# The first requests of a one-core LSTM kernel: four steps of x, a part of Wx, then the other four steps

## The chip, the cores and the metric

The kernel runs on one core of a Trainium2 chip. The metric is the device time of one execution in microseconds (us), lower is better. A core has a matrix engine (TensorE, PE in the profile, with PEld for its weight loads), a vector engine (VectorE, DVE), a scalar engine (ScalarE, ACT), a general one (GpSimd, POOL) and a synchronising one (SyncE, SP). SP, ACT and POOL also issue the transfers (DMAs) from main memory.

## The reference

A sequence x of 64 steps for 32 sequences (256 features) goes through an LSTM with 256 hidden units, then through a feed-forward network with weights of plus and minus one, and the result is added to x. All is float32.

```python
xW = jnp.einsum('ntd,dg->ntg', x, Wx) + b
def step(carry, xw_t):
    prev_h, prev_c = carry
    a = xw_t + prev_h @ Wh
    i = jax.nn.sigmoid(a[:, :Hd])
    f = jax.nn.sigmoid(a[:, Hd:2 * Hd])
    o = jax.nn.sigmoid(a[:, 2 * Hd:3 * Hd])
    g = jnp.tanh(a[:, 3 * Hd:])
    next_c = f * prev_c + i * g
    next_h = o * jnp.tanh(next_c)
    return ((next_h, next_c), next_h)
...
h = jnp.concatenate([x, -x], axis=-1)
h = s0 * _conn_dense(k0, h)
h = jax.nn.relu(h) * 2
h = s1 * _conn_dense(k1, h)
h = jax.nn.relu(h) * 2
h = s2 * _conn_dense(k2, h)
...
x = x + _L0_ffn_ref(_L0_cond_ref(x, cond_1024, ...), ...)
```

Here x of the second part is the hidden state of every step, and Hd is 256.

## The kernel before, in words

**The steps of the LSTM.** The 64 steps are a recurrence: each needs the hidden state of the one before. For each step TensorE multiplies the state with Wh (`gates_from_h`, L301 to 312: 32 matrix instructions on the trace, since a float32 product is two passes), ScalarE and VectorE do the cell (`cell_step`, L319 to 342), and VectorE turns the new state round for the next product. While the cell is worked out, TensorE does work that does not depend on it: in the first 21 steps the products of x with Wx for later steps (`x_products`, L272), then the feed-forward network of steps already done (`ffn_block`, L585, and `last_block`, L417). So TensorE always has a queue of work, and the program's order on it is fixed by the loop over t at the end of the function.

**Layout.** A step's gates lie on 128 partitions as four groups (q) of 32 sequences, each with 64 of the 256 hidden units. Wx and Wh are each 256 rows by 1024 columns and stand in SBUF as two chunks of 128 rows (k = 0, 1) and four slots of 256 columns. `GATES = (3, 0, 1, 2)` says which gate of the reference stands in which slot: slot 0 is g, slots 1, 2 and 3 are i, f and o. `load_gates` (L118) asks for some slots of some chunks; with two engines given, each asks for one half of the partitions. `load_x` (L88) asks for eight steps of x (a half of a block of 16), or a part of them, in four transfers, one for each q. `turn_x` (L226) turns them round on VectorE.

**The start.** This is where the change lies. VectorE zeroes `warm` (L108, 40 words a partition), `idle` (L110, 512 bf16 values, done as 256 words) and the two tiles `b_row` (L116) into which the bias goes. TensorE first multiplies `idle` with itself: two products that put zeros into the two banks of the gates (L641) and `WARM_UP` = 8 into a bank that nothing reads (L643, `p_idle`). Then come, in this order on TensorE:

1. `x_part` (L242, its matmul is L246) for steps 0 to 7 with chunk 0 and slots 1 and 2: the first pass;
2. the same with slots 0 and 3: the second pass;
3. the bias, spread over the partitions by a product (`copy_bias`, L658), which needs `b_row`;
4. chunk 1 with all slots for steps 0 to 7; after each two steps VectorE moves the sum, with the bias, to SBUF (`evict_x`, L262);
5. the products for steps 8 to 11, which need the second eight steps of x, turned on VectorE after the first `evict_x`;
6. the first recurrence, which needs Wh and the turned initial state `h_first` (L679).

**The requests.** SP and ACT ask for the large tiles, in the order of the program: the first eight steps of x (q0 and q2 by SP, q1 and q3 by ACT), Wx chunk 0 (slots 1 and 2 in one request by SP, slot 0 and slot 3 by ACT), Wx chunk 1 in the same way, the second eight steps of x, then Wh. The requests of these two engines share eight semaphores in turn. A request takes the semaphore of the one that stands eight places ahead of it, so it waits on its engine until that one has landed, and what is behind it on the same engine waits too. POOL asks for `h_first`, for three pieces of the bias and for the three scales, and then computes with the scales (L169 to L183). After these SP alone asks for more of x (L155), k0 (L162) and k1 (L198).

Of the kernel before, what the change touches and what calls it, by code (L numbers as in the profile page):

```python
# [32 lines left out]
F32 = mybir.dt.float32  # L33
# [8 lines left out]
def lstm_ffn(ctx: ExitStack, tc: tile.TileContext, x, cond, wx_d, wh_d, b_d, k0_d, k1_d, k2_d, s0_d, s1_d, s2_d, out):  # L42
    nc = tc.nc
    P = 128
# [3 lines left out]
    NQ = 4  # L48
    HQ = H // NQ
# [3 lines left out]
    SB = 16  # L53
    NB = T // SB
    TB = SB * N
# [6 lines left out]

    FIRST_CHORE = 2
    W2_STEP = 24
    WARM_UP = 8

    SUM_STEP = 28

    const = ctx.enter_context(tc.tile_pool(name="const", bufs=1))
# [12 lines left out]
    def act(shape, dtype, name):  # L82
        return apool.tile(shape, dtype, tag="act", name=name)
# [4 lines left out]
    def load_x(i, half, engines, part=slice(0, SB // 2)):  # L88
        if part.start == 0:
            xq[i, half] = xpool.tile([P, SB // 2, HQ], F32, tag="x", name=f"x{i}_{half}")  # L90
        t0 = i * SB + half * (SB // 2)
        for q in range(NQ):
            engines[q % len(engines)].dma_start(
                out=xq[i, half][q * N : (q + 1) * N, part],
                in_=x[:, t0 + part.start : t0 + part.stop, ts(q, HQ)],
            )
# [5 lines left out]
    wx = wpool.tile([P, 2, G], F32, tag="wx", name="wx")  # L102
# [2 lines left out]
    w2 = const.tile([P, 2, FC1, P], F32R, name="w2")  # L105

    warm = const.tile([P, 40], F32, name="warm")
    nc.vector.memset(warm, 0.0)  # L108
    idle = const.tile([P, 512], mybir.dt.bfloat16, name="idle")
    nc.vector.memset(idle, 0.0)  # L110

    first = warm[:, 4 : 4 + N]
    nc.vector.memset(first[:1], 1.0)
# [4 lines left out]
    def load_gates(t, w_d, slots, engines, chunks=slice(0, 2)):  # L118

        w_rows = w_d.rearrange("(p b) g -> p b g", b=2)  # L120
        s0, n, g0 = slots[0], len(slots), GATES[slots[0]]
        if len(engines) == 1:
            halves = [slice(0, P)]
        else:
            halves = [slice(0, P // 2), slice(P // 2, P)]
        for engine, half in zip(engines, halves):
            engine.dma_start(
                out=t[half, chunks, s0 * H : (s0 + n) * H], in_=w_rows[half, chunks, g0 * H : (g0 + n) * H]
            )


    both = [nc.sync, nc.scalar]
    load_x(0, 0, both)
    for k in range(2):
        load_gates(wx, wx_d, (1, 2), [nc.sync], slice(k, k + 1))
        for slot in (0, 3):
            load_gates(wx, wx_d, (slot,), [nc.scalar], slice(k, k + 1))
    load_x(0, 1, both)
    load_gates(wh, wh_d, (1, 2), both)
    load_gates(wh, wh_d, (0,), [nc.scalar])  # L140
    load_gates(wh, wh_d, (3,), [nc.sync])

    nc.scalar.activation(warm[:, 1:2], warm[:, :1], AF.Sigmoid)
    h_first = const.tile([P, HQ], F32, name="h_first")
    nc.gpsimd.dma_start(out=h_first, in_=cond.rearrange("n (q j) -> q n j", q=NQ))
    b_rows = b_d.rearrange("(o g h) -> o g h", o=1, g=4)
    nc.gpsimd.dma_start(out=b_row[0][:1, :1], in_=b_rows[:, 3:])
    nc.gpsimd.dma_start(out=b_row[0][:1, 1:], in_=b_rows[:, :1])
    nc.gpsimd.dma_start(out=b_row[1][:1], in_=b_rows[:, 1:3])
    scales = []  # L150
    for i, s_d in enumerate((s0_d, s1_d, s2_d)):
        s = const.tile([P, 1], F32, name=f"s{i}")
# [73 lines left out]
    def turn_x(i, half, part=slice(0, SB // 2)):  # L226
        if part.start == 0:
            xT[i, half] = act([P, SB // 2, 2, N], F32, f"xT{i}_{half}")
        nc.vector.transpose(
            xT[i, half][:, part], xq[i, half][:, part].rearrange("p t (j b) -> p t b j", b=2)  # L230
        )
# [405 lines left out]
    outputs = deque()  # L637

    p_idle = ps_f.tile([P, TB], F32, tag="pf", name="p_idle")
    for g in gate_banks:  # L640
        nc.tensor.matmul(g, idle[:, :P], idle, start=True, stop=True)  # L641
    for n in range(WARM_UP):
        nc.tensor.matmul(p_idle, idle[:, :P], idle, start=True, stop=True)  # L643
    turn_x(0, 0, slice(0, SB // 4))
    turn_x(0, 0, slice(SB // 4, SB // 2))
    for i in range(4):
        load_bits(i)
    for half in range(2):
# [53 lines left out]
    for t in range(T):  # L702
# [22 lines left out]
        else:  # L725
            if t >= FIRST_CHORE and chores:
                part = chores.popleft()()
# [40 lines left out]
```

## Time and profile before

| what | value |
|---|---|
| median of 3 runs | 312.36 us (312.21 to 312.55) |
| the profiled execution's own time | 312.31 us |
| its span on the core | 310.5 us |
| TensorE busy | 304.5 us, 98% of the span |
| share of TensorE in the chain that ended last | 97% |
| first instruction on TensorE | at 1.24 us |
| first product of x | at 5.44 us |
| first product of the recurrence | at 16.60 us |

The times of one instruction and of its group come from the profiled execution, counted from the start of its span. A matmul is pipelined, so its time in the profile (634 ns for a product of zeros) is longer than the distance from one to the next (0.43 us); for the length of a run of matmuls the distance counts. The chain of work that ended last is followed back from the last instruction: what stands on it sets the end. A weight load can start before the matmul ahead of it is done.

### The profile page before, as it was taken

How to read it: one execution, taken by the hardware profiler on the slowest of the kernel's cores; microseconds unless marked ns; L12 is line 12 of the kernel's file. 1: busy time of each engine (PE TensorE's matmuls, PEld its weight loads, DVE VectorE, ACT ScalarE, POOL GpSimd, SP SyncE). 2: the span in 40 equal slices, each digit the busy share in tenths (PEclk: the TensorE clock that was granted, in tenths of full speed). 3: DMA queues.
4: the chain of work that ended last, by engine and by line, in shares of the span. 5: the costliest groups of instructions: out<-in, count | busy, mean ns of one | idle time of the engine just before them, and what ended most of it. 6: DMA issues, size and time to landing. Idle time of an engine off the chain costs nothing.

```text
span 310.5 us, 9798 instructions
## 1 busy us (share of the span) xinstructions
PE 304.5 (98%) x4138; PEld 242.7 (78%) x4138; DVE 178.1 (57%) x530; ACT 142.0 (46%) x512; POOL 6.6 (2%) x24
## 2 busy tenths in 40 slices
PE   8999999999999999999999999999999999999994
PEld 4888888788777777777777777777777777899993
DVE  2566767777673444355754445567554434698543
ACT  0225566774564543435633434355443333886220
POOL 5300000000000000000000000000000000000000
PEclk9999999999999999999999999999999999999999
DMA  6874001142000000000010000000310000131002
GB/s 192 206 196 99 5 19 38 36 95 65 3 2 0 2 2 0 3 2 0 2 38 22 14 3 0 2 2 13 92 34 2 3 0 2 31 79 27 2 0 69
DMA packets 30587, 10.89 MB, mean 35 GB/s; under 512 B 27720, under 2 KB 29768, under 8 KB 30544
## 3 DMA queue, kind: packets, MB, share of 16 engines
q1 hardware_dynamic: 27136, 8.66, 11.2%
q10 hardware_dynamic: 3168, 1.57, 2.0%
q8 instruction: 32, 0.52, 0.7%
q0 software_dynamic: 240, 0.04, 0.1%
q14 instruction: 11, 0.09, 0.1%
HBM read 8.16 MB, written 2.10 MB: 33 GB/s over the span
## 4 chain that ended last, share of the span: by engine, by line
PE 97%; DVE 1%; ACT 0%; issue 0%; ACTq 0%
PE p L617 30%; PE gates L305 20%; PE px L246 18%; PE p L591 8%; PE po L604 7%; PE gates L452 4%; PE po L561 2%; PE r L452 2%; PE x L452 2%; PE p L479 2%; PE p_idle L643 1%; PE gates L641 0%; DVE a_7l L362 0%; DVE o L388 0%; PE p_bias L658 0%
## 5 line engine op out<-in xcount | busy, mean ns | idle before, releaser
L305 PEld LDWEIGHTS gates<-wh,hist 128*32 128x32 f32 x2016 | 54.6, 109 | 22.3 <-issue 13.4
L305 PE MATMUL gates<-wh,hist 128*32 128x192 f32 x2016 | 68.1, 275 | 0.0
L246 PE MATMUL px<-wx,xT 128*32 128x256 f32 (+1 forms) x1168 | 60.5, 353 | 0.1
L322 ACT ACTIVATE sig<-gates 128x128 f32<-128x128 f32 x64 | 17.7, 277 | 80.6 <-PE gates L305 80.4
L246 PEld LDWEIGHTS px<-wx,xT 128*32 128x32 f32 x1168 | 42.4, 110 | 11.3 <-DVE c_first L652 0.7
L326 DVE TENSOR_TENSOR kept<-sig,c 128x64 f32<-128x64 f32 x63 | 14.2, 225 | 50.0 <-ACT sig L322 49.7
L332 ACT ACTIVATE th<-c 128x64 f32<-128x64 f32 x64 | 16.4, 257 | 31.4 <-DVE c L330 31.4
L334 DVE TENSOR_TENSOR h<-sig,th 128x64 f32<-128x64 f32 x64 | 14.4, 225 | 20.7 <-ACT th L332 20.7
L262 DVE TENSOR_TENSOR xg<-px,bias 128x512 f32<-128x512 f32 x32 | 21.2, 671 | 2.8 <-PE px L246 2.3
L316 ACT COPY gates<-xg 128x192 f32<-128x192 f32 x64 | 20.0, 313 | 1.3 <-DVE xg L262 1.3
L591 PE MATMUL p<-hhi,w 128*128 128x512 f32 x48 | 19.3, 402 | 0.0
L591 PE MATMUL p<-hlo,w 128*128 128x512 f32 x48 | 19.1, 398 | 0.0
L339 DVE STREAM_TRANSPOSE hist<-h 128x64 f32<-128x64 f32 x64 | 15.7, 245 | 2.4
L330 DVE TENSOR_TENSOR c<-kept,new 128x64 f32<-128x64 f32 x64 | 14.4, 224 | 2.2
L324 ACT ACTIVATE sig<-gates 128x64 f32<-128x64 f32 x64 | 14.9, 233 | 0.1
L323 ACT ACTIVATE cand<-gates 128x64 f32<-128x64 f32 x64 | 14.0, 218 | 0.0
L328 DVE TENSOR_TENSOR new<-sig,cand 128x64 f32<-128x64 f32 x64 | 13.9, 217 | 0.0
L317 ACT COPY gates<-xg 128x64 f32<-128x64 f32 x64 | 13.0, 203 | 0.0
L591 PEld LDWEIGHTS p<-hhi,w 128*128 128x128 f32 x48 | 9.0, 188 | 2.2
L591 PEld LDWEIGHTS p<-hlo,w 128*128 128x128 f32 x48 | 9.0, 188 | 2.0
L211 ACT ACTIVATE w<-bits,nsgn,sgn 128x1024 fp32r<-128x1024 uint8 x8 | 9.9, 1241 | 0.0
L617 PE MATMUL p<-a_7h,w 128*128 128x512 f32 x24 | 9.9, 413 | 0.0
(249 smaller groups left out, 602.8 us busy)
## 6 DMA issues: line engine op xcount, KB each, us to landing
x<-in_x_dram SPq DMA_DIRECT2D x60, 64.0 KB, 2.8
out_dram<-o SPq DMA_DIRECT2D x28, 64.0 KB, 1.8
bits<-in_L_ffn_k_dram SPq DMA_DIRECT2D x10, 128.0 KB, 3.2
wx<-in_L_cond_Wx_dram SPq DMA_DIRECT2D x2, 256.0 KB, 4.2
wx<-in_L_cond_Wx_dram ACTq DMA_DIRECT2D x4, 128.0 KB, 4.6
wh<-in_L_cond_Wh_dram ACTq DMA_DIRECT2D x2, 256.0 KB, 5.6
wh<-in_L_cond_Wh_dram SPq DMA_DIRECT2D x2, 256.0 KB, 6.2
k<-in_L_ffn_k_dram SPq DMA_DIRECT2D x2, 256.0 KB, 3.1
```

What stands on the lines that cost most here:

```text
L246: nc.tensor.matmul(p[q * N : (q + 1) * N, t % 2, slots], xT[i // 2, i % 2][:, s, k, :], wx_q[:, k, q, slots], start=start, stop=False, ski ...
L262: nc.vector.tensor_tensor(xg[t], p.rearrange("p t g j -> p t (g j)"), b, ALU.add)
L305: nc.tensor.matmul(g[q * N : (q + 1) * N], hT[:, k, :], wh_q[:, k, q, slots], start=False, stop=(k == 1), skip_group_check=True,)
L316: nc.scalar.copy(gates[0], x_t[:, :3])
L322: nc.scalar.activation(sig[:, 0:2, :], gates[0][:, 1:3], AF.Sigmoid)
L324: nc.scalar.activation(sig[:, 2, :], gates[1][:, 0], AF.Sigmoid)
L332: nc.scalar.activation(th, c, AF.Tanh)
L339: nc.vector.transpose(hT, h.rearrange("p (j b) -> p b j", b=2))
L452: nc.tensor.matmul(bank[pair][:, i], a(k)[:, ts(2 * pair + i, P)], b(k, n), start=first and i == 0 and k == 0 and n == 0, stop=last and k ...
L591: nc.tensor.matmul(p, w0[:, k, ts(m, P)], a[:, k, :], start=(n == 0), stop=(n == 3))
L604: nc.tensor.matmul(po[m], w2[:, m, k], a1[k][n], start=(k == 0 and n == 0), stop=(k == FC1 - 1 and n == 1))
L617: nc.tensor.matmul(p1[m], w1[:, k, ts(m, P)], a0[k][n], start=(k == 0 and n == 0), stop=(k == FC0 - 1 and n == 1),)
```

## The change

Four things change, all before the first product.

- `idle` is 128 columns instead of 512 and is zeroed before `warm`; a product of zeros reads its 128 columns four times over, so that it still has 512 columns. `WARM_UP` is 7 instead of 8.
- The first eight steps of x are asked for in two parts of four steps. Between them stands Wx chunk 0, slots 1 and 2, now in two halves of the partitions, one by SP and one by ACT.
- After the second part come slot 3 (SP) and slot 0 (ACT) of chunk 0, then chunk 1: slots 1, 2 and 3 in one request by SP, slot 0 by ACT.
- On POOL the three requests for the bias come before that for `h_first`.

The two turns of x on VectorE were in parts of four steps before as well.

```diff
-    WARM_UP = 8
+    WARM_UP = 7
...
     warm = const.tile([P, 40], F32, name="warm")
+    idle = const.tile([P, P], mybir.dt.bfloat16, name="idle")
+    nc.vector.memset(idle, 0.0)
     nc.vector.memset(warm, 0.0)
-    idle = const.tile([P, 512], mybir.dt.bfloat16, name="idle")
-    nc.vector.memset(idle, 0.0)
...
     both = [nc.sync, nc.scalar]
-    load_x(0, 0, both)
-    for k in range(2):
-        load_gates(wx, wx_d, (1, 2), [nc.sync], slice(k, k + 1))
-        for slot in (0, 3):
-            load_gates(wx, wx_d, (slot,), [nc.scalar], slice(k, k + 1))
+    first_x = [slice(0, SB // 4), slice(SB // 4, SB // 2)]
+    load_x(0, 0, both, first_x[0])
+    load_gates(wx, wx_d, (1, 2), both, slice(0, 1))
+    load_x(0, 0, both, first_x[1])
+    load_gates(wx, wx_d, (3,), [nc.sync], slice(0, 1))
+    load_gates(wx, wx_d, (0,), [nc.scalar], slice(0, 1))
+    load_gates(wx, wx_d, (1, 2, 3), [nc.sync], slice(1, 2))
+    load_gates(wx, wx_d, (0,), [nc.scalar], slice(1, 2))
     load_x(0, 1, both)
...
-    h_first = const.tile([P, HQ], F32, name="h_first")
-    nc.gpsimd.dma_start(out=h_first, in_=cond.rearrange("n (q j) -> q n j", q=NQ))
     b_rows = b_d.rearrange("(o g h) -> o g h", o=1, g=4)
...
     nc.gpsimd.dma_start(out=b_row[1][:1], in_=b_rows[:, 1:3])
+    h_first = const.tile([P, HQ], F32, name="h_first")
+    nc.gpsimd.dma_start(out=h_first, in_=cond.rearrange("n (q j) -> q n j", q=NQ))
...
+    zeros = idle.unsqueeze(1).to_broadcast([P, TB // P, P])
     for g in gate_banks:
-        nc.tensor.matmul(g, idle[:, :P], idle, start=True, stop=True)
+        nc.tensor.matmul(g, idle, zeros, start=True, stop=True)
     for n in range(WARM_UP):
-        nc.tensor.matmul(p_idle, idle[:, :P], idle, start=True, stop=True)
-    turn_x(0, 0, slice(0, SB // 4))
-    turn_x(0, 0, slice(SB // 4, SB // 2))
+        nc.tensor.matmul(p_idle, idle, zeros, start=True, stop=True)
+    for part in first_x:
+        turn_x(0, 0, part)
```

## The prediction

> **What bounds the kernel now.** I read the page's busy table first, then the chain of work that ended last in order of time, then the timeline of the first 8 us, then the landings of the first requests.
>
> ```profile
> span 310.5 us, 9798 instructions
> PE 304.5 (98%) x4138; PEld 242.7 (78%) x4138; DVE 178.1 (57%) x530; ACT 142.0 (46%) x512; POOL 6.6 (2%) x24
> ```
>
> TensorE is busy in 98% of the span. What is missing is the 1.24 us before its first instruction and the tail, so a microsecond saved at the start is a microsecond saved at the end, unless a wait opens later. The chain of the first 17 us (start, length, what):
>
> ```profile
> 0.91 0.28 DVE idle L110
> 1.19 0.05 issue
> 1.24 1.03 PE gates L641 x2
> 2.27 3.23 PE p_idle L643 x8
> 5.51 1.89 PE px L246 x64
> 7.39 0.12 issue
> 7.51 1.96 PE px L246 x64
> 9.47 0.47 PE p_bias L658 x16
> 9.94 6.91 PE px L246 x128
> 16.84 0.83 PE gates L305 x28
> ```
>
> It runs: memset of `idle`, ten matmuls of zeros, first pass of Wx (chunk 0, slots 1 and 2), a wait of 0.12, second pass (chunk 0, slots 0 and 3), bias, chunk 1 and four more steps, first recurrence. The zeros, not a transfer, end just before the first pass. The timeline shows it:
>
> ```profile
> 4.20 0.15 PEld L643 LDWEIGHTS <-idle 128*128 128x128 bf16 x1 [0.28 <-issue]
> 4.32 0.77 DVE L229 STREAM_TRANSPOSE xT<-x 128x256 f32<-128x256 f32 x2 [2.02 <-DMA x<-in_x_dram]
> 4.63 0.15 PEld L643 LDWEIGHTS <-idle 128*128 128x128 bf16 x1 [0.28 <-issue]
> 5.07 0.11 DVE L652 MEMSET c_first<- 128x64 f32 x1
> ```
>
> One zero takes 0.43 us (4.20 to 4.63). Both transposes of x are done at 5.09 and the first weights at 5.06 (next fence), while the first px instruction starts at 5.44, when the last zero is through. The group of the zeros:
>
> ```profile
> L643 PE MATMUL p_idle<-idle x8: 454/634/634, 2.1 to 5.1; 128*128 128x512 bf16 x8
> ```
>
> Seven zeros last 634 ns, the one that starts at 5.05 only 454: TensorE's clock rises there. The same 512 columns are 0.23 us apart at 201 us, against 0.43 here, so until then work costs 1.87 times as much. The shorter zero saved 0.18 of the possible 0.20, so the rise comes soon after 5.05; I take 5.2. Landings, asked for one request at a time (issues at 1.66, 2.19 and 3.16):
>
> ```profile
> wx<-in_L_cond_Wx_dram SPq DMA_DIRECT2D x1, 256.0 KB, 3.4
> wx<-in_L_cond_Wx_dram ACTq DMA_DIRECT2D x1, 128.0 KB, 5.2
> wx<-in_L_cond_Wx_dram ACTq DMA_DIRECT2D x1, 128.0 KB, 4.5
> ```
>
> The first holds slots 1 and 2 (lands 5.06); the second, slot 3, lands at 7.39: it is the 0.12 us wait.
>
> **The sum's base.** The profiled execution took 312.31 us: a span of 310.5 and 1.81 around it. The median of the runs shown is 312.36, 0.05 above; I subtract from each.
>
> **Part 1, the memset.** `idle` shrinks from 256 words to 64 and goes ahead of `warm`. A row with 64 words of 128 partitions is c_first, 0.11 us, against 0.27 now; `warm` (0.09 us) is no longer in front. The zeros start at 0.82 + 0.11 + 0.06 = 0.99 instead of 1.24: 0.25 gained. `warm`, `first` and b_row follow on VectorE; b_row ends 0.2 earlier, as all of them are shorter together.
>
> **Part 2, one zero fewer.** One cadence: 0.43 us. Nine zeros from 0.99 end at 0.99 + 9 x 0.427 = 4.83.
>
> **Part 3, the zeros read 128 columns four times over.** No row shows a matmul with a repeated moving operand. The columns are 512 as before, which excludes a gain. The nearest row is the second pass, whose operand comes in two pieces: 1.96 against 1.89 us, 4%, on nine zeros 0.15 us. I take 0, as the column count sets the cadence, and keep 0.15 for the range.
>
> **Part 4, the requests.** Instead of 18 requests up to the end of wh there are 22: eleven by SP (eight before) and eleven by ACT (ten); four more at about 0.44 us of queue each. There are eight semaphores for them, and each request past the eighth waits until the one eight places ahead has landed; so SP issued nothing between 2.58 and 4.14 in the trace. Beyond that neither queue has anything to do for TensorE but the copies to the gate banks on ACT, at 11.56 now, with the table load (1.28 us) in between; ACT's last early request goes when chunk 1 has landed, about 8, as now (8.11), so the table is there by about 10 again.
>
> What the first pass needs: the first x parts (32 KB each, issued at 0.73 to 1.2). The 64 KB ones took 2.2 to 2.9 us; the halves land by 3.1 (at worst 4.1, today's last), and the transpose, 0.45, ends by 3.7 (4.6). Slots 1 and 2 go in two halves from both queues at about 1.66, in place of one. With 3.4 us as today they land at 5.06, with less x ahead of them nearer 4.3. The first of these would put the first pass at 5.15, the second leaves it to the zeros at 4.83. I take 4.83 and keep 5.15.
>
> Two queues for one piece: today's x parts on SP and ACT together filled the engines (mean share 1.04 from 2 to 4 us), so halves win no bandwidth. The Trainium skill, "DMA: Bandwidth & Descriptors", rules for kernel authors, says that two transfers to disjoint halves of the partitions aren't worth it, as they share the same engines; by that rule the pair lands no sooner than one request would, and only the smaller x ahead of it counts. The sum by it would be 0.3 us less, the case of 5.15 above.
>
> **The clock on the first pass.** From 4.83 to 5.2 px runs slow: 0.37 x (1 - 0.23/0.43) = 0.17 lost. The pass lasts 1.95 now (5.44 to 7.39), so it ends at 4.83 + 0.17 + 1.95 = 6.95. If the rise moves with the first zero (0.25 earlier), the loss is 0.06.
>
> The Trainium skill, "TensorE: Matmul & The Clock Gate", Part 1 (The HAM clock gate), speaks against fewer zeros: the clock is held at half until a free-running window of some 3.4 us has been busy, seen about 4 us into the work, and it recommends 4 us of warming. Nine zeros are 3.84 us. By its 4 us the rise would come at 4.99, and the sum would be 0.1 better than mine; by its window at its worst, two windows after 0.99, px would stay slow to 7.8 and the change would lose about 0.7.
>
> **The second pass** needs slots 0 and 3 by 6.95. They now wait for the second x parts of the first four, so they are issued at about 3.15, later than today's 1.69 and 2.19, but with x and 256 KB of wx ahead instead of that and 256 KB of chunk 1 besides. At 3.4 us (the lightly loaded row) they land at 6.55, at 4.5 (the row issued at 3.16) at 7.65, at 5.2 at 8.35. Behind 230 KB of backlog rather than some 750 I take the first: no wait, and the 0.12 goes. The second half of x, requests seven to ten, is issued by 2.8; with 2.9 it lands at 5.7, turned by 6.15 at worst against t = 4 at 6.0: hidden to 0.15.
>
> **Chunk 1** now waits for the halves of slots 1 and 2, so it is issued at 4.3 to 5.1, not 2.15 to 3.54, and with 3.4 to 5.0 us lands between 7.7 and 10.1. TensorE wants it at 6.95 + 1.96 + 0.47 = 9.38. I take about 8.2, nothing.
>
> **POOL's order.** b_row goes first and waits for its memset (about 1.6), and lands earlier than today's 7.9. h_first is issued at about 3.1 instead of 1.25 and with 4.0 us lands at 7.1; it is turned at 14.04. The scales go some 0.4 later: their POOL work ends near 11.7 and the first reader is at 25.02. All hidden; cover gone, h_first costs nothing before 13. x(0,1) (turned at 11.45), wh (wanted at 16.84, lands 14.9 now) and the x, k0 and bits behind them on SP move by less than their 1.9 us or more of slack.
>
> **Sum.** The second pass starts at 6.95 instead of 7.51: 0.56. So 312.31 - 0.56 = 311.75 for an execution like the profiled one, 311.80 for the median. 0.2% of it, 0.62 us, is about what a measurement can tell from no change: my value lies just inside.
>
> **Rivals.**
> - *Slots 0 and 3 come as late as today.* For it: they are asked for 1 to 1.5 us later, and the row issued at 3.16 took 4.5. Against: a third of the bytes ahead. At 4.5 the second pass starts at 7.75, 0.24 later than now: 312.6; the edge where nothing is won is a landing at 7.39. Chunk 1 at 10.1 would likewise cost 0.7 and end at 312.5.
> - *The clock rises late (slower).* Nine zeros might not do, or px with its waits not count as work. If it took another 3.96 us (today's first zero to rise) from 4.83, px would lose 3.96 x 0.465 = 1.84 against a gain of 0.73 (5.44 - 4.83 + 0.12): 313.5. Equality is at a rise at 6.4, 0.2% slower at 7.7. Against: px follows the zeros without a gap.
> - *All goes early.* Rise with the first zero, px at 4.80: 0.25 + 0.43 + 0.12 less 0.06 = 0.74: 311.6.
> - *The change doesn't do what it says:* the first pass waits for wx at 5.15, gain 0.41: 311.95; taken into the first case.
>
> **How the numbers follow.** Forecast with its spread (311.65 to 312.0) 0.57; late slots or chunk 1 0.20; late clock 0.07; all early 0.16. Faster by 0.2% (under 311.74) are the last and about 0.4 of the first: 0.40. Slower (over 312.98) are the late clock and a quarter of the late slots: 0.12. Within: 0.48. The range leaves out the late clock and the worst of the late slots above, and little below: 311.4 to 312.6.
>
> **What would show it.** Right: first zero at 0.99, first px near 4.83, no wait between the passes, first recurrence near 16.3, 0.56 less span. Wrong: px starting after its wx landing (over 4.9); a wait ahead of the second pass or of chunk 1; px weight loads at the slow cadence beyond 5.2; or TensorE idle between 12 and 17 us for x or wh.

## The result, and the profile after

The changed kernel took 315.2 us (median of 6 runs, 314.36 to 317.58), the kernel before 312.47 us (6 runs, 312.21 to 313.07). The ratio is 1.0101, with a 95% interval of 1.0062 to 1.014; here and in the experiments the ratio lies within 0.0004 of that of the means of the runs, while the two medians alone would give 1.0088. The changed kernel is slower by 1.0%; the forecast was 311.8 us, and its range ended at 312.6.

The profiled execution of the changed kernel took 314.36 us, the shortest of the six, with a span of 312.6 us, 2.0 more than before (312.57 against 310.53). The head of its page:

```profile
span 312.6 us, 9802 instructions
PE 305.0 (98%) x4137; PEld 240.4 (77%) x4137; DVE 178.3 (57%) x530; ACT 142.2 (45%) x512; POOL 6.6 (2%) x24
```

TensorE's busy time hardly moved (304.5 to 305.0), so the span grew by time in which TensorE stood still. The chain of work that ended last, in the first 19 us (start, length, what), says where:

```profile
0.68 0.06 issue
0.73 0.43 ACTq L93
1.16 0.03 issue
1.19 0.45 ACTq L93
1.64 0.03 issue
1.67 3.31 DMA wx<-in_L_cond_Wx_dram
4.98 0.02 issue
5.00 6.40 DMA wx<-in_L_cond_Wx_dram
11.40 0.04 issue
11.45 7.11 PE px L249 x128
18.56 0.87 PE gates L308 x32
```

Before, this chain was all TensorE from 1.24 on. Now its first 11.4 us are transfers, one behind the other. ACT's half of slots 1 and 2 is asked for at 1.67 and lands at 4.98. At 5.00 ACT issues the request for chunk 1, slot 0, which had waited for that landing, and it lands 6.40 us later, at 11.40. Only then does TensorE start chunk 1. The timeline shows the same from the engines' side (start, length, engine and line, operation, tile and sizes, in brackets the idle time before and what ended it):

```profile
0.99 1.04 PE L645 MATMUL gates<-idle 128*128 128x512 bf16 x2 [0.99 <-DVE warm L110]
...
3.53 1.39 SPq L127 DMA_DIRECT2D wx<-in_L_cond_Wx_dram  x2
...
3.78 1.57 ACTq L127 DMA_DIRECT2D wx<-in_L_cond_Wx_dram  x2
...
5.07 4.34 PE L249 MATMUL px<-wx,xT 128*32 128x128 f32 x128
...
9.22 0.66 PE L662 MATMUL p_bias<-b_row,warm 128*32 128x128 f32 x16
...
11.45 1.93 PE L249 MATMUL px<-wx,xT 128*32 128x256 f32 x31 [1.57 <-DMA wx<-in_L_cond_Wx_dram]
```

The zeros start at 0.99, the first pass at 5.07, and both passes are one group of 128 matmuls with a gap of only 0.04 us, at 6.55, where the weights for step 4 waited for the second turn of x. All of that is what the change was said to do. The bias begins at 9.22. Then TensorE is idle for 1.57 us, until 11.45. The four wx issues of SP and ACT between 3.53 and 5.35 are slots 3 and 0 of chunk 0 and then chunk 1; within each pair the second is the one for chunk 1 (issued at 4.56 and 5.00).

What the chunk 1 requests took, from the DMA view of this kernel for issues from 4.5 to 5.2 us (KB each, us from issue to landing):

```profile
wx<-in_L_cond_Wx_dram SPq DMA_DIRECT2D x1, 384.0 KB, 6.6
wx<-in_L_cond_Wx_dram ACTq DMA_DIRECT2D x1, 128.0 KB, 6.4
```

In the kernel before, chunk 1 was asked for at 2.15, 3.16 and 3.54 and had landed by 8.09. From its DMA view, the parts issued at 2.15 and at 3.54:

```profile
wx<-in_L_cond_Wx_dram SPq DMA_DIRECT2D x1, 256.0 KB, 5.0
wx<-in_L_cond_Wx_dram ACTq DMA_DIRECT2D x1, 128.0 KB, 4.6
```

**The balance.** TensorE had done the bias and was ready for chunk 1 at 9.94 before and at 9.88 now (0.06 gained). The wait costs 1.57. Chunk 1 and the four steps after it take 7.11 us instead of 6.91 (0.20): behind the wait their first product no longer overlaps the bias (before, it started at 9.70 and the bias ended at 9.94). Together 1.71; the first recurrence begins 1.72 later on the chain (18.56 against 16.84). TensorE's lag stays at that to the end: its last product ends 1.79 later on the chain (307.74 against 305.95). The remaining quarter of a microsecond of the span's 2.0 stands behind the last instruction of VectorE, where only the output is written.

The median is another 0.8 above the profiled execution, and no profile was taken of a longer one. Each run's mean granted clock is on record, though: 0.991 and 0.992 in the two longest (317.04 and 317.58), 0.995 to 0.998 in the other four, and never under 0.996 in the runs of the kernel before beside the experiments. A stretch of 3.4 us at half clock, as the profile of one experiment below shows after a wait, lowers the mean by 0.005. So these two executions probably had such a stretch on top of the wait; no trace shows it.

### The profile page after: what moved, and what is told of

Same layout as the page of the kernel before. It is cut to its first block, busy times and chain, and to the rows that moved or that the text cites. A ratio compares the mean times of both kernels' runs of the same rounds, so it can differ in the third digit from the quotient of the medians.

```text
span 312.6 us, 9802 instructions
## 1 busy us (share of the span) xinstructions
PE 305.0 (98%) x4137; PEld 240.4 (77%) x4137; DVE 178.3 (57%) x530; ACT 142.2 (45%) x512; POOL 6.6 (2%) x24
## 3 DMA queue, kind: packets, MB, share of 16 engines
q1 hardware_dynamic: 27248, 8.79, 11.4%
## 4 chain that ended last, share of the span: by engine, by line
PE 94%; DMA 3%; DVE 1%; ACTq 0%; ACT 0%; issue 0%
PE p L620 30%; PE gates L308 20%; PE px L249 17%; PE p L594 8%; PE po L607 7%; PE gates L455 4%; DMA wx<-in_L_cond_Wx_dram 3%; PE po L564 2%; PE r L455 2%; PE x L455 2%; PE p L482 2%; ACTq L93 0%; DVE a_7l L365 0%; DVE o L391 0%; DVE o L388 0%
## 5 line engine op out<-in xcount | busy, mean ns | idle before, releaser
L249 PEld LDWEIGHTS px<-wx,xT 128*32 128x32 f32 x1168 | 40.4, 111 | 15.6 <-DMA wx<-in_L_cond_Wx_dram 1.8
```

What stands on the lines that cost most here:

```text
L249: nc.tensor.matmul(p[q * N : (q + 1) * N, t % 2, slots], xT[i // 2, i % 2][:, s, k, :], wx_q[:, k, q, slots], start=start, stop=False, ski ...
```

## The experiments

**Theories.** The lateness theory: chunk 1 stands as requests 13 and 14 behind eight shared semaphores. The first eight requests hold only 448 KB (four x parts of 32 KB, two halves of 128 KB, two x parts of 32 KB), where the first eight held 1024 KB before, a part of chunk 1 among them. So it is asked for only when the halves of slots 1 and 2 have landed, and lands late. Its rivals: the one wide request of slots 1, 2 and 3 (rows of 3 KB) is slow in itself; the halves are; the shorter warm-up or POOL's order did it. Every ratio below is against runs of the kernel before on the same chip, with its 95% interval.

### One part of the change at a time

The zeros alone (memset of 128 columns, nine products, repeated reading):

```diff
-    WARM_UP = 8
+    WARM_UP = 7
...
-    nc.vector.memset(warm, 0.0)
-    idle = const.tile([P, 512], mybir.dt.bfloat16, name="idle")
+    idle = const.tile([P, P], mybir.dt.bfloat16, name="idle")
     nc.vector.memset(idle, 0.0)
+    nc.vector.memset(warm, 0.0)
...
-        nc.tensor.matmul(p_idle, idle[:, :P], idle, start=True, stop=True)
+        nc.tensor.matmul(p_idle, idle, zeros, start=True, stop=True)
```

> The kernel before with the smaller memset and nine zeros, its requests and POOL's order untouched. If the zeros end the start of the first pass, as the profile of before shows, the first pass starts at about 5.1 (its weights land at 5.06, the turn of x ends at 5.09) instead of 5.44, but the second pass still waits for slot 3 at 7.39: so the chain gives back nearly all, 0.0 to 0.15 us faster than before. If one zero fewer lets the clock rise later, up to 1.5 us slower. If this part were what made the changed kernel slow, about 2.7 us slower.

Measured: 312.81 us (12 runs), ratio 1.002 (1.0001 to 1.0039). The chain of this kernel:

```profile
1.67 3.83 DMA wx<-in_L_cond_Wx_dram
5.50 0.14 issue
5.63 3.99 PE px L246 x128
```

The first pass starts at 5.63, when slots 1 and 2 have landed (5.50), and not when the zeros end: what the zeros gain is lost to a transfer that is no sooner. Chunk 1, asked for at 2.15 to 3.5, landed by 8.49 and was not waited for. The medians hardly differ (312.81 against 312.78); the ratio comes from four long runs, which the run with eleven zeros below takes up.

The requests alone:

```diff
-    load_x(0, 0, both)
-    for k in range(2):
-        load_gates(wx, wx_d, (1, 2), [nc.sync], slice(k, k + 1))
-        for slot in (0, 3):
-            load_gates(wx, wx_d, (slot,), [nc.scalar], slice(k, k + 1))
+    load_x(0, 0, both, first_x[0])
+    load_gates(wx, wx_d, (1, 2), both, slice(0, 1))
+    load_x(0, 0, both, first_x[1])
+    load_gates(wx, wx_d, (3,), [nc.sync], slice(0, 1))
+    load_gates(wx, wx_d, (0,), [nc.scalar], slice(0, 1))
+    load_gates(wx, wx_d, (1, 2, 3), [nc.sync], slice(1, 2))
+    load_gates(wx, wx_d, (0,), [nc.scalar], slice(1, 2))
```

> The kernel before with the new order and sizes of the requests alone. If the requests make chunk 1 late by themselves (theory: asked for late, behind the landing of the halves of slots 1 and 2), 2 to 3.5 us slower than before, with a wait of 1.5 us or more of TensorE for wx after the bias. If it takes POOL's new order as well (theory: h_first and the scales collide with chunk 1), within 0.6 us of before, chunk 1 landing before 9.5.

Measured: 314.81 us (4 runs), ratio 1.0086 (1.0053 to 1.012). The chain:

```profile
5.74 6.30 DMA wx<-in_L_cond_Wx_dram
12.04 0.04 issue
12.09 7.11 PE px L249 x128
```

The order of the requests alone brings the loss and the same wait: the last part of chunk 1 is asked for at 5.74 and takes 6.30 us.

POOL's order alone:

```diff
-    h_first = const.tile([P, HQ], F32, name="h_first")
-    nc.gpsimd.dma_start(out=h_first, in_=cond.rearrange("n (q j) -> q n j", q=NQ))
     b_rows = b_d.rearrange("(o g h) -> o g h", o=1, g=4)
...
     nc.gpsimd.dma_start(out=b_row[1][:1], in_=b_rows[:, 1:3])
+    h_first = const.tile([P, HQ], F32, name="h_first")
+    nc.gpsimd.dma_start(out=h_first, in_=cond.rearrange("n (q j) -> q n j", q=NQ))
```

> The kernel before with the bias asked for ahead of h_first on POOL. Theory of the requests: no difference, within 0.3 us of before, wx chunk 1 landing near 8.1. Theory of POOL's order: chunk 1 lands later than 8.1 and the kernel is slower, by up to 2.7 us if this alone is the cause.

Measured: 312.62 us (10 runs), ratio 1.0 (0.9986 to 1.0013). It does nothing that can be measured. The three parts by themselves make 0.2, 0.86 and 0.0%, together about the 1.01% of the whole change.

### What in the requests it is

Chunk 1 in three requests, as before, in the changed kernel:

```diff
-    load_gates(wx, wx_d, (1, 2, 3), [nc.sync], slice(1, 2))
-    load_gates(wx, wx_d, (0,), [nc.scalar], slice(1, 2))
+    load_gates(wx, wx_d, (1, 2), [nc.sync], slice(1, 2))
+    for slot in (0, 3):
+        load_gates(wx, wx_d, (slot,), [nc.scalar], slice(1, 2))
```

> The changed kernel with chunk 1 in three requests as before (slots 1 and 2 by SP, slots 0 and 3 by ACT) in place of three slots in one by SP. If the one wide request of 384 KB with rows of 3 KB is what lands late, chunk 1 lands by 9.4 and the kernel is 2 us or more faster than the changed one, near 312. If it is late because it is asked for late, it lands at 11 or later and the kernel stays at 314.5 to 317.

Measured: 315.11 us (4 runs), ratio 1.0077 (1.0062 to 1.0092). Asked for at 4.68, 5.14 and 5.65, the three landed at 9.25, 10.77 and 11.85. The wide request is not the cause: without it chunk 1 is as late.

Slots 1 and 2 in one request again:

```diff
-    load_gates(wx, wx_d, (1, 2), both, slice(0, 1))
+    load_gates(wx, wx_d, (1, 2), [nc.sync], slice(0, 1))
```

> The changed kernel with slots 1 and 2 of chunk 0 in one request by SP instead of two halves. Theory of the eight places: one place is won, chunk 1 still waits for the landing of wx and of x, so 314 to 316 as the changed kernel. Rival, the halves share their engines and hinder each other: 312.5 or less.

Measured: 316.33 us (4 runs), ratio 1.0111 (1.0073 to 1.0148). The halves are not the cause either. They also win nothing: in the profiles the one request landed at 4.97, the later of the two halves at 4.98.

The first x in four whole requests, as before, and all else as changed:

```diff
-    load_x(0, 0, both, first_x[0])
+    load_x(0, 0, both)
     load_gates(wx, wx_d, (1, 2), both, slice(0, 1))
-    load_x(0, 0, both, first_x[1])
```

> The changed kernel with the first eight steps of x asked for whole again, so four requests fewer; the halves of slots 1 and 2, nine zeros and POOL's order stay. Theory of the eight places (small requests fill the eight places, 448 KB under way instead of 1024, and push chunk 1 behind the landing of wx): the first eight now hold 768 KB, chunk 1 waits for the first x alone, is asked for at about 3.1 and lands by 8.5; no wait for it, 312.0 to 312.7. Rival, the halves of wx or the 384 KB request: still a wait of 1 us or more for chunk 1, 314 or more.

Measured: 313.13 us (12 runs), ratio 1.002 (1.0007 to 1.0034). With four requests fewer, chunk 1 was asked for at 2.90 and 3.16, had landed by 8.59, and nothing waited for it: four fifths of the loss are gone. What is left in the profiled execution stands elsewhere in the chain:

```profile
2.29 5.86 DMA wx<-in_L_cond_Wx_dram
8.14 0.04 issue
8.19 1.96 PE px L248 x64
10.14 0.47 PE p_bias L661 x16
10.62 6.91 PE px L248 x128
```

This is slot 0 of chunk 0, asked for at 2.29 and landed only at 8.14, and the second pass behind it, 0.68 us later than before (8.19 against 7.51). Now everything is asked for early and the piece that is needed second comes late. This kernel also has the nine zeros, which alone measured the same 1.002; which of the two the 0.2% of all runs come from is not settled.

The other way to ask for chunk 1 early: the second four steps of x behind it.

```diff
     load_gates(wx, wx_d, (1, 2), both, slice(0, 1))
-    load_x(0, 0, both, first_x[1])
...
     load_gates(wx, wx_d, (0,), [nc.scalar], slice(1, 2))
+    load_x(0, 0, both, first_x[1])
```

> The changed kernel with the second four steps of x asked for after chunk 1. Theory of the eight places: chunk 1 is now requests nine and ten, asked for at about 3, and lands by 8.5 without a wait; the second part of x is asked for at 3.8 to 5.5 and lands at about 7, so the first pass waits for it at its step 4, about 1 us: 312.3 to 313.5. Rival, the transfers are slow between 6 and 11 us whatever is asked for when: chunk 1 lands after 10, 314 or more.

Measured: 318.71 us (4 runs), ratio 1.0196 (1.0183 to 1.0209); the upper end of the expectation was missed by 5 us. Chunk 1, asked for at 2.86 and 3.13, landed by 7.99, as the theory has it. But x, asked for at 5.52, took until 9.79 and stood on the chain in its place:

```profile
5.52 4.27 DMA x<-in_x_dram
...
9.98 0.46 DVE xT L232
10.44 0.04 issue
10.49 4.31 PE px L249 x96
```

And the standstill had a price of its own. The windows of this kernel, one us each (busy us of PE, PEld, DVE, ACT and POOL with instruction counts, then the granted TensorE clock, the DMA share and GB/s):

```profile
8.00:9.00 1.00, 0.00 (x0) 0.00 (x0) 0.00 (x0) 0.00 (x0) 0.00 (x0) 1.00 0.19 39
9.00:10.00 1.00, 0.00 (x0) 0.00 (x0) 0.02 (x1) 0.00 (x0) 0.53 (x3) 1.00 1.07 238
10.00:11.00 1.00, 0.51 (x12) 0.48 (x16) 0.51 (x2) 0.59 (x1) 0.76 (x5) 0.58 0.92 280
...
12.00:13.00 1.00, 1.00 (x24) 0.94 (x20) 0.00 (x0) 0.00 (x0) 0.22 (x2) 0.50 0.91 243
13.00:14.00 1.00, 1.00 (x36) 0.95 (x32) 0.00 (x0) 0.00 (x0) 0.00 (x0) 0.72 1.10 345
```

TensorE has nothing to do from 7.2 to 10.5; the clock (the third number from the end) falls in the window from 10, is 0.50 in that from 12 and rises again in that from 13. By the clock's records it was at half from 10.2 to 13.6. All four runs of this kernel have a mean granted clock of 0.987 to 0.991, lower than any run of the kernel before.

The opposite test, in the kernel before: chunk 1 behind the second eight steps of x and nothing else.

```diff
             load_gates(wx, wx_d, (slot,), [nc.scalar], slice(k, k + 1))
-    load_x(0, 1, both)
+        if k == 0:
+            load_x(0, 1, both)
```

> The kernel before with chunk 1 asked for after the second eight steps of x; requests as large as before. Theory that it is enough to be asked for late: chunk 1 is asked for at 4 to 6 us and lands at 10.5 or later, 1 to 3 us slower than before. Theory that the few bytes under way of the small requests are needed too (768 KB here in the first eight, 448 in the changed kernel): chunk 1 lands by 9.5, and the kernel is within 0.6 us of before.

Measured: 313.89 us (4 runs), ratio 1.0043 (1.0027 to 1.0059). The chain:

```profile
6.00 0.35 ACTq L127
6.36 0.04 issue
6.40 3.86 DMA wx<-in_L_cond_Wx_dram
10.25 0.14 issue
10.39 7.11 PE px L247 x128
```

Both theories missed in part: the kernel lost, as the first has it, but chunk 1 landed at 10.25. (The first eight requests hold 832 KB here, not the 768 of the expectation.) Being asked for late is enough to lose, but less than half of what the change loses. Here the last part of chunk 1 was asked for at 6.40, later than in the changed kernel, and took 3.86 us, not 6.40. So the loss has two parts: the late request, and a latency that is 2.5 us longer behind the new order. The two latencies are of requests of the same size (128 KB), but 256 KB of chunk 1 had been asked for at 3.33 here, while in the changed kernel all of it came after 4.5.

### Where the long latency is from

Two suspects that run beside chunk 1 in the changed kernel were tried: POOL's requests for the scales (128 rows of 4 bytes each) were left out, and the requests for the second eight steps of x were moved behind a part of Wh.

```diff
-        nc.gpsimd.dma_start(out=s, in_=s_d.partition_broadcast(P))
+        nc.gpsimd.memset(s, 0.03125)
```

> The changed kernel with the three scales set by a memset on POOL instead of being requested; the scales' values are left out, so its output is not the reference's. Theory that the small requests of POOL hold up transfer engines just when chunk 1 moves (they land between 6.9 and 12.4 in the changed kernel): chunk 1 lands by 9.5, no wait or a short one, 312.5 or less. Theory that being asked for late is all: chunk 1 still lands at 10.5 or later, 314 to 317.

Measured: 313.99 us (10 runs), ratio 1.004 (1.0026 to 1.0054). The chain:

```profile
5.27 0.02 issue
5.29 5.67 DMA wx<-in_L_cond_Wx_dram
10.96 0.04 issue
11.01 7.37 PE px L249 x125
```

The last part of chunk 1 still takes 5.67 us, 0.73 less than in the changed kernel. The profiled execution was the longest of the ten (315.5 us), so it is not the typical one. The ratio is lower than that of the changed kernel by 0.6%, and the intervals do not meet (1.0054 against 1.0062), so the requests for the scales probably have a part in the loss; none of these ten runs has a mean clock under 0.996, against two of the six of the changed kernel. But without them chunk 1 was still late and waited for.

```diff
-    load_x(0, 1, both)
     load_gates(wh, wh_d, (1, 2), both)
+    load_x(0, 1, both)
```

> The changed kernel with slots 1 and 2 of Wh asked for ahead of the second eight steps of x. Theory that the 256-byte rows of x, asked for behind chunk 1, take its turns on the transfer engines: chunk 1 lands by 9.5 and the kernel is 312.5 to 313.5. Theory that being asked for late is all: chunk 1 lands at 10.5 or later, 314 to 317, and the second eight steps of x come later too.

Measured: 317.15 us (4 runs), ratio 1.0138 (1.0121 to 1.0155). Chunk 1 was asked for at 4.59 and 5.05 and landed at 12.08 and 12.36, later still; in addition x for steps 8 to 15 landed at 15.56 and was waited for. So chunk 1 is late without these x requests right behind it too; but Wh stands there in their place, so the run does not show what chunk 1 would take with nothing behind it. The packet records of the changed kernel say more: from 6.5 to 8.0 us the data packets on the queues of SP and ACT were chunk 1's alone (of 3 KB and 1 KB, its rows). The first 256-byte packet of x behind it started at 8.11, the first 2-KB packet of Wh at 10.23. Neither moved in the first stretch in which chunk 1 was slow.

The cause of the long latency stays open. What the trace shows is in the DMA view of the changed kernel and of the kernel before, 0 to 12 us in 40 slices of 0.3 us, each digit the busy share of the 16 transfer engines in tenths. The changed kernel:

```profile
DMA  0000007352598799687999843446897466699999
```

The kernel before:

```profile
DMA  0000004999999668999999788444978989996999
```

From 2.1 to 3.3 us the changed kernel's engines are 0.2 to 0.5 busy (3, 5, 2, 5 after the first 7) where those of before are full; the eight semaphores are taken by small requests then. Counted from the packets, 1008 KB had moved by 7.5 us, against 1428 KB before. From 6.9 to 8.1 us (4, 3, 4, 4) the changed kernel's are more than half idle again although all of chunk 1 has been asked for. The kernel before has such a valley too, from 7.5 to 8.4 us (4, 4, 4), but there chunk 1 has all but landed. Within the request of 384 KB the first engine was done at 7.53 and the last at 11.19, and by the packet records single packets of 3 KB took up to 1.5 us, against a median of 0.12 us. So the engines fall out of step with each other. What holds single packets up is not shown.

### Can parts of it be kept?

Slot 3 of chunk 0 by SP ahead of chunk 1, in the kernel before, alone:

```diff
-    for k in range(2):
-        load_gates(wx, wx_d, (1, 2), [nc.sync], slice(k, k + 1))
...
+    load_gates(wx, wx_d, (1, 2), [nc.sync], slice(0, 1))
+    load_gates(wx, wx_d, (0,), [nc.scalar], slice(0, 1))
+    load_gates(wx, wx_d, (3,), [nc.sync], slice(0, 1))
+    load_gates(wx, wx_d, (1, 2), [nc.sync], slice(1, 2))
```

> The kernel before with slot 3 of chunk 0 asked for by SP ahead of chunk 1's slots 1 and 2, and nothing else. A try for a kernel that beats both. If the wait for slot 3 before the second pass is what the requests can still give, that wait (0.12 us in the profile of before) goes: 0.1 to 0.3 us faster. If chunk 1, asked for some 1 us later, becomes the wait: 0.2 to 1 us slower.

Measured: 312.58 us (12 runs), ratio 0.9996 (0.9986 to 1.0006): no difference. The same with the nine zeros and POOL's order of the change (the diffs of both are above):

> The same with the changed kernel's nine zeros, small memset and POOL order. If the requests were the whole fault of the change, this is the version with the rest of its gain: 0.1 to 0.5 us faster than before. If the first pass waits for slots 1 and 2 anyway, the shorter zeros are worth nothing: within 0.3 us of the run without them.

Measured: 314.27 us (9 runs), ratio 1.0036 (1.0019 to 1.0053), slower. The requests were not the whole fault, then: with POOL's order at 1.0, the nine zeros are the suspect. The profiled execution is the shortest of the nine (313.05), so no trace shows what the others lost.

What the warm-up is worth: `WARM_UP = 0` in the kernel before, so two products of zeros instead of ten.

> The kernel before with the two products that zero the gate banks and none of the eight idle ones: the price of the zeros. If the clock rises a fixed time of about 4 us after the first work of TensorE, whatever it is, no loss; the first pass starts at about 5.1, 0 to 0.3 us faster. If it takes a full stretch of unbroken work, px runs slow from 5.1 to 8.6 or later, 1.6 to 3 us slower, and one zero fewer can cost something when a transfer leaves a gap behind the zeros.

Measured: 314.65 us (4 runs), ratio 1.006 (1.0036 to 1.0083). The chain of this kernel has

```profile
6.34 5.15 PE px L246 x128
```

where that of the kernel with slot 3 first, whose passes start at the same 6.34, has

```profile
6.34 3.70 PE px L248 x128
```

The same 128 matmuls take 1.45 us longer. In the trace's clock records the full clock comes at 9.36 in the first and at 3.98 in the second.

The small memset and the repeated reading with eleven zeros instead of nine (`WARM_UP = 9`):

> The kernel before with the small memset, the zeros that read 128 columns four times, and eleven zeros in place of ten (nine in the changed kernel); requests and POOL's order untouched. If a gap between the zeros and the first pass is what costs 0.2% with nine zeros (TensorE idle for a while, the clock rising later on average), eleven close it and the kernel is 0 to 0.5 us faster than before. If the repeated reading or the memset itself cost something, it is 0.2% or more slower like the run with nine. If neither matters, within 0.1%.

Measured: 312.39 us (11 runs), ratio 0.9995 (0.9986 to 1.0004). The memset and the repeated reading cost and win nothing. Against it the nine zeros of the first experiment were 0.25% slower, with intervals that only touch. The 12 runs of the nine zeros lie in two groups, eight at 312.2 to 313.0 and four at 314.2 to 315.0; the 11 runs of the eleven zeros all lie between 311.98 and 312.80. The first record of full clock lasts a whole multiple of 3.41 us in all 16 profiles. A clock that rises 3.41 us later in a third of the executions would cost these about 1.6 us (an estimate: at half clock work takes 1.87 times as long, so 3.41 x 0.465), most of the 2 us between the groups. But no profile fell into the upper group, so it is not shown; the mean clocks can't show it, since the time before the first record counts as full (1.000 in the profile without warm-up, where the rise comes at 9.36).

No version was measurably faster than the kernel before.

## Why the prediction was wrong

**The step that failed: "Chunk 1 now waits for the halves of slots 1 and 2, so it is issued at 4.3 to 5.1 ... and with 3.4 to 5.0 us lands between 7.7 and 10.1. ... I take about 8.2, nothing."** The mechanism and the issue times were right: 4.56 and 5.00. The term that was mis-sized is the latency: 6.6 and 6.4 us, so 11.19 and 11.40 instead of 8.2, and past the upper end too. The bounds were the rows of before for pieces of wx, all of them asked for by 3.6 us. In the kernel before with chunk 1 moved back these bounds hold (3.86 us for a request at 6.40); behind the new order they don't, in six kernels of six with split x and a late chunk 1 (the last part landed 5.67 to 7.30 us after its request). What makes the latency longer there stays open.

Rows that would have warned stood in the profile of before, on requests that nothing waited for: two parts of Wh, asked for at 8.11. From the DMA view of the kernel before, issues from 8.1 to 8.2 us:

```profile
wh<-in_L_cond_Wh_dram SPq DMA_DIRECT2D x1, 256.0 KB, 6.8
wh<-in_L_cond_Wh_dram ACTq DMA_DIRECT2D x1, 256.0 KB, 6.6
```

They move as much as chunk 1 together and have other large requests around them, as chunk 1 has at its new place. With 6.8 us the bound for chunk 1, from its latest issue at 5.1, would have been 11.9 instead of 10.1, and its price 2.5 us (against the 9.38 at which it was wanted) instead of 0.7.

**The case for it was in the text and not carried on.** Part 4 counted the eight semaphores and the requests in the ring, but not their bytes: 448 KB in the first eight instead of 1024 KB. The transfer engines were at a mean share of 1.03 between 2 and 3.5 us before, and at 0.51 now. "A third of the bytes ahead" was read as shorter queues for what follows; it was also transfer time that is lost: by 7.5 us 1008 KB had moved instead of 1428. The same miss moved what stands behind chunk 1 on ACT: its table load, expected to be done by about 10, ended at 13.30, though TensorE did not wait for it.

**Part 1 and 2, the zeros: right in time, but they end in front of a transfer.** The zeros started at 0.99, as worked out, and the last one ended about 4.81 (seven from 1.82, 0.427 apart). The first pass started at 5.07 and not at 4.83, because slots 1 and 2 landed at 4.98; the other value that the text kept, 5.15, was the nearer one. (For that case the text has two sums: "0.3 us less" under part 4, and a gain of 0.41 instead of 0.56 among the rivals, which is 0.15 less. The second is right, as a later start runs less at half clock.) As a part by itself the zeros gained nothing: 1.002. The rule of the Trainium skill, "DMA: Bandwidth & Descriptors", rules for kernel authors, that two transfers to disjoint halves aren't worth it, was the better guide: one request landed at 4.97, two halves at 4.98.

That landing is also not as fixed as one profile made it look. In the eight kernels of this study that ask for the first x and for slots 1 and 2 as the kernel before does (itself one of them), slots 1 and 2 landed between 5.02 and 6.20 us. The profile of before (5.02; the text's 5.06 adds the rounded 3.4) was at the early end, so its "the zeros, not a transfer, end just before the first pass" holds for that execution and not for all.

**Part 3, the repeated reading: right.** Nothing (the eleven zeros, 0.9995).

**The clock on the first pass: smaller matter, wrong time.** The rise came at 5.93 by the clock records, not at 5.2. Both passes took 4.15 us (5.07 to 9.22) where the working made 4.08 of them (4.83 to 8.91), so the size was right within 0.1. Across the kernels of this study the rise came between 3.98 and 9.36 us and did not keep a fixed distance from the first zero. The Trainium skill, "TensorE: Matmul & The Clock Gate", Part 1 (The HAM clock gate), calls the window free-running, which agrees with such a scatter (2.7 to 6.0 us after the first zero in the 15 profiles with nine zeros or more, a spread of about one stretch of 3.41 us); the text weighed this and still took one time from one profile.

**The second pass: right.** Slots 3 and 0 landed at 6.53 and 6.70 (forecast 6.55), the second half of x by 6.06, turned by 6.53. TensorE waited 0.04 us for that turn; the text had it hidden to 0.15. In the profile of the requests alone the same wait was 0.60 us (6.89 to 7.49); chunk 1 was later still there, so it cost nothing by itself. The rival that these come late fell in the changed kernel; it came true when x was asked for whole (8.14).

**POOL's order, the bias, `h_first`: right.** Nothing on TensorE waited for them, and the order alone measured 1.0.

**The rival of the late clock** gave 313.5 by another way. It is not what made the profiled execution slow: that has 1.57 us of waiting for chunk 1, and the passes at the expected length. For other executions it is not excluded: four of the twelve runs of the nine zeros alone were about 2 us longer than the rest.

## What to carry to other kernels

When requests share a fixed number of semaphores, cutting the first ones into small pieces also cuts the bytes in flight: add up the bytes of the first eight, and ask which large piece is pushed past the eighth and when it can be asked for at all. A latency may be taken from the profile of before only for a request at the same place in the same order; for a moved one, price the worst case beyond every row and compare it with the slack of the piece, not only with the slack of the piece that the change wants early. A gain at an engine's start is worth only what the transfer that ends next leaves of it, and one profile gives that transfer's landing with a scatter of a microsecond.

## What the runs showed of the hardware that I had not expected

- Chunk 1 (512 KB) with its last request between 3.1 and 3.6 us had landed by 8.0 to 8.95 in all nine profiles of such kernels. With the last request at 5.0 to 5.7, behind split x, it landed at 10.9 to 12.4, in six of six: the landing moved by more than the request.
- The 16 engines of one request can end up to 3.7 us apart (7.53 to 11.19), while their mean share in the first part of that time (7.53 to 8.1) is about 0.4.
- After some 3.3 us without work in one execution, TensorE's granted clock was at half for 3.4 us (10.2 to 13.6). After waits of 1.57 and 2.24 us (the profiles of the changed kernel and of Wh ahead of x) it stayed full.
- Eight products of zeros at the start are worth 0.6% of the whole run (1.0036 to 1.0083), though nothing reads them.
